# The second half's expert rows: gathered into buffers of their own and added by VectorE, instead of accumulated into x by the gather

## The chip, the cores and the metric

One NeuronCore of one Trainium2 chip runs one program. The metric is the device time of one execution in microseconds (us). Shorter is better.

## The reference, cut to what matters

Two transformer layers work on x of 8 batches by 512 tokens by 128 features, all in float32. Layer 0 adds to x a causal attention of 16 heads and a mixture of experts: every token goes to 6 of 32 experts, and a shared expert serves all. Layer 1 adds a second causal attention (4 heads) and a chain of three blocks of dense layers with a layer norm and a gelu.

```python
x = L0_attn_x
xn = _layernorm(x, axis=-1)
x = x + _L0_attn_ref(xn, ...) + _L0_ffn_ref(xn, ...)
xn = _layernorm(x, axis=-1)
x = x + _L1_attn_ref(xn, ...) + _L1_ffn_ref(xn, ...)

# in _L0_ffn_ref, TOP_K = 6
_, top_idx = jax.lax.top_k(corrected, TOP_K)
combine = jnp.zeros((T, E), x.dtype).at[jnp.arange(T)[:, None], top_idx].add(top_w)
out = jnp.einsum('teh,te->th', y, combine) + shared_out
```

Only the last sum of the mixture is touched here: for each token the weighted outputs of its six experts are added to x.

## The kernel before, in words

x stays on the chip as eight tiles `x_b[b]`, one for each batch, of 128 partitions by 4 token tiles by 128 features. The mixture is done in two halves of four batches each (`TH` = 16 token tiles a half). In each half GpSimd first scatters the rows of the normalised tokens to DRAM, grouped by expert (`scatter`, L605). `expert_slots` then works through them in 16 groups of 8 slots of 128 rows, and writes the weighted outputs to the DRAM tensor `ys[h]` (L691). Last, `gather` (L695) fetches them back: one indirect DMA of GpSimd brings, for a token tile `t` and a choice `k` of the six, 128 rows of 128 floats, and accumulates them into `x_b[b][:, tb, :]` in flight (`compute_op=ALU.add`). A half has 16 x 6 = 96 such gathers, ordered by batch, then choice, then token tile.

The order of the work is written by hand (`manual_schedule`): each engine executes its instructions in the order in which the program issues them. The main loop (L1138) runs over 193 ticks (`T1`), the steps of the change's title. Three ticks do the attention of a pair of heads: 64 pairs. In a tick stand, in this order: the scores of the next tick, the jobs planned for place 0, the exponentials, the transposes of the tick before, the jobs of place 1, a projection, in each third tick `values` (L512, the matmuls `yps`), and the jobs of places 2 and 3. `plan(tick, place, job)` puts a job into that order. After the loop a second one over `u` does layer 1, and works off the jobs of ticks `T1 + u`.

What is planned around the change:

- The second half's expert slots end at tick 145. Its gathers start at tick 149 (`FIRST_SLOTS[1] + APART * NG + 2` = 99 + 48 + 2), place 3, two a tick, and so end at tick 196. The first half's start at tick 101, three a tick.
- `output` (L580) adds batch b's attention to `x_b[b]`: 72 matmuls `z` on TensorE, then one VectorE instruction (L594). It is planned for place 3 of tick 24 (b + 1) + 13: 157 for batch 5, 181 for batch 6. Batch 7's stands at tick 194.
- `prepared(b)` (L831) brings x to layer 1 in eight steps: statistics on VectorE, powers and products on GpSimd (L153, L842, L845, L856, L874, L892, L899), transposes and projections on TensorE. Batches 0 and 1 are prepared from tick 150 on, a step every four ticks, at place 2 (`EARLY_AT`). The others come later; batch 4 starts at tick 195.
- `norm` (L1019) of the dense blocks also has its powers and products on GpSimd (L153, L1031).
- `divide` (L559) multiplies an attention output by its divisors on VectorE (L561, 128x512).
- `evacuate` (L157) gives each copy out of PSUM to VectorE or ScalarE, whichever has the smaller sum in `load_of`.
- `pp` is a pool of SBUF tiles that opens at tick 148, after the expert slots.

Of the kernel before, what the change touches and what calls it, by code (L numbers as in the profile page):

```python
# [10 lines left out]
F32 = mybir.dt.float32  # L11
# [3 lines left out]
ALU = mybir.AluOpType  # L15
AX = mybir.AxisListType

P = 128
B, L, D = 8, 512, 128
NT = L // P  # L20
# [9 lines left out]
TH = TT // NH  # L30
# [3 lines left out]
NG = NS // GS  # L34
FIRST_SLOTS, APART = (51, 99), 3
# [14 lines left out]
def kernel(ctx: ExitStack, tc: tile.TileContext, a: dict, out: bass.AP):  # L50
    nc = tc.nc
# [22 lines left out]
    rows = ctx.enter_context(tc.tile_pool(name="rows", bufs=1, space=bass.MemoryType.DRAM))  # L74
# [8 lines left out]
    x_b, x_in = [], a["x"].rearrange("b (t p) d -> b p t d", p=P)  # L83
# [47 lines left out]
    xs, ys = [], []  # L131
# [23 lines left out]
    load_of = {"dve": 0.0, "act": 0.0}  # L155
# [54 lines left out]
    index = w0.tile([P, TT, TOP_K], U32, name="index")  # L210
# [403 lines left out]
    def expert_slots(h, g):  # L614
# [77 lines left out]
            out=ys[h][at : at + GS * P].rearrange("(s p) d -> p s d", p=P), in_=yg  # L692
        )

    def gather(t, k):  # L695
        b, tb = divmod(t, NT)
        nc.gpsimd.indirect_dma_start(  # L697
            x_b[b][:, tb, :], None, ys[t // TH],
            bass.IndirectOffsetOnAxis(index[:, t, k : k + 1], 0), compute_op=ALU.add,
        )  # L700

    experts = ExitStack()

# [3 lines left out]
    def plan(tick, place, job, *args):  # L707
        beside.setdefault((tick, place), []).append((job, args))
# [33 lines left out]
    for h in range(NH):  # L742
        for g in range(NG):
            first = FIRST_SLOTS[h] + APART * g
            parts = expert_slots(h, g)

            for tick, place in ((-4, 3), (-3, 1), (-1, 1), (0, 2), (1, 3)):
                plan(first + tick, place, next, parts, None)
        moves = [
            (t, k) for b in range(h * B // 2, (h + 1) * B // 2) for k in range(TOP_K)  # L750
            for t in range(b * NT, (b + 1) * NT)
        ]
        for i, (t, k) in enumerate(moves):
            at = i // 3 if h == 0 else i // 2
            plan(FIRST_SLOTS[h] + APART * NG + 2 + at, 3, gather, t, k)

# [379 lines left out]
    for tick in range(T1):  # L1138
# [23 lines left out]
        if tick == FIRST_SLOTS[-1] + APART * NG + 1:  # L1162
            experts.close()
            token_rows[0].close()
            pp = later_pools.enter_context(tc.tile_pool(name="prep1", bufs=1, side="right"))
# [65 lines left out]
```

## Time and profile before

| | |
|---|---|
| time, median of 14 runs | 1391.99 us (1384.06 to 1399.53) |
| profiled execution's own time | 1393.89 us |
| its span, first to last instruction | 1392.2 us |
| mean granted TensorE clock | 0.904 of full speed |
| busy: TensorE / VectorE / ScalarE / GpSimd | 82% / 55% / 53% / 49% of the span |
| chain that ended last | PE 59%, issue 13%, POOL 13%, DVE 7%, DMA 2% |
| of it POOL, gathers (L697) | 7% |
| gathers, both halves | 192, 301.2 us busy on GpSimd |
| scatters, both halves | 192, 186.0 us busy on GpSimd |

The engines stand in the profile as PE (TensorE), DVE (VectorE), ACT (ScalarE), POOL (GpSimd) and SP (the engine whose queue issues most DMAs). [...] A group of instructions is written "line engine operation, output<-input". An idle time in square brackets is the time in which the engine stood still just before an instruction, with what ended it.

### The profile page before, as it was taken

To read this page: it belongs to the slowest core of one execution; us is meant where nothing else is said; L and a number is where in the kernel's file an instruction comes from. 1 tells how busy PE (TensorE), PEld (TensorE's weight loads), DVE (VectorE), ACT (ScalarE), POOL (GpSimd) and SP (SyncE) were. 2 spreads that over 40 slices of the span, in tenths; PEclk is the share of its full clock that TensorE was granted. 3 is DMA by queue.
4 is the path that set the end of the run, shared out by engine and by line. 5 is a ranking of instruction groups with operands and counts; after the bars stand their busy time and mean duration, and the time that the engine had idled before them with its cause. 6 is when DMAs were issued, how large, how long until landed. Compare 5 with 4: busy or idle time off the path is not lost.

```text
span 1392.2 us, 25274 instructions
## 1 busy us (share of the span) xinstructions
PE 1135.7 (82%) x8534; PEld 751.8 (54%) x8534; DVE 760.1 (55%) x2563; ACT 743.5 (53%) x1977; POOL 681.0 (49%) x738
## 2 busy tenths in 40 slices
PE   5897423942249999999999999999999777888896
PEld 2554211421225676667666666766656545665564
DVE  4572311600016656675665566566667357687885
ACT  4475211610006665675665566566556356677785
POOL 2037477187750000000058888402888878866651
PEclk9899655865559999999999999999999989999999
DMA  9529212131111465676679889852324224000000
GB/s 286 143 53 270 83 59 82 53 94 58 57 43 42 137 183 150 165 201 174 160 179 238 193 191 224 209 159 65 49 31 87 29 28 88 13 9 16 8 9 23
DMA packets 204052, 151.05 MB, mean 108 GB/s; under 512 B 17682, under 2 KB 192276, under 8 KB 203924
## 3 DMA queue, kind: packets, MB, share of 16 engines
q1 hardware_dynamic: 166340, 119.51, 31.5%
q0 software_dynamic: 36864, 28.34, 11.1%
q10 hardware_dynamic: 720, 1.61, 0.3%
q8 instruction: 67, 1.10, 0.3%
q14 instruction: 61, 0.50, 0.1%
HBM read 93.52 MB, written 55.87 MB: 107 GB/s over the span
## 4 chain that ended last, share of the span: by engine, by line
PE 59%; issue 13%; POOL 13%; DVE 7%; another core or an unknown queue 3%; DMA 2%; ACT 2%; SPq 0%; ACTq 0%; DVEq 0%; POOLq 0%
PE sc L457 11%; PE pt_ps L501 9%; PE yps L524 9%; POOL x L697 7%; PE qk_ps L427 7%; PE z L585 4%; PE v_ps L438 3%; PE ye_ps L679 2%; POOL rn L153 2%; PE xt_ps L655 2%; PE u_ps L667 2%; PE g_ps L667 2%; DVE neg L923 2%; PE pt_ps L956 1%
## 5 line engine op out<-in xcount | busy, mean ns | idle before, releaser
L697 POOL DMA_INDIRECT x<-ys,index x192 | 301.2, 1569 | 428.7 <-DMA ys<-yg 302.4
L465 DVE CUSTOM_DVE_ANT_0 neg<-sc,mask 128x512 f32<-128x512 f32 (+3 forms) x512 | 225.3, 486 | 166.6 <-PE sc L457 87.6
L480 ACT ACTIVATE neg<-neg,nmax 128x512 f32<-128x512 f32 (+3 forms) x512 | 281.3, 554 | 22.5 <-DVE nmax L465 22.3
L169 ACT COPY pT<-pt_ps 128x512 f32<-128x512 f32 x283 | 156.3, 585 | 256.2 <-PE pt_ps L501 179.7
L457 PE MATMUL sc<-qkT 64*128 64x384 f32 (+3 forms) x1024 | 206.1, 478 | 42.7 <-DVE nmax L465 21.8
L605 POOL DMA_INDIRECT xs<-xe,index x192 | 186.0, 969 | 62.0 <-issue 35.3
L501 PE MATMUL pt_ps<-ident,neg 128*128 128x128 f32 x1280 | 189.2, 287 | 26.6 <-issue 15.7
L501 PEld LDWEIGHTS pt_ps<-ident,neg 128*128 128x128 f32 x1280 | 141.0, 144 | 105.5 <-issue 55.0
L524 PE MATMUL yps<-pT,vs 128*64 128x128 f32 (+1 forms) x1792 | 162.0, 327 | 33.4 <-issue 27.4
L524 PEld LDWEIGHTS yps<-pT,vs 128*64 128x64 f32 x1792 | 113.1, 139 | 118.2 <-issue 63.2
L457 PEld LDWEIGHTS sc<-qkT 64*128 64x128 f32 x1024 | 91.7, 192 | 145.2 <-issue 58.4
L585 PE MATMUL z<-wz_sb,yT 128*128 128x128 f32 x512 | 80.0, 291 | 74.0 <-issue 72.8
L585 PEld LDWEIGHTS z<-wz_sb,yT 128*128 128x128 f32 x512 | 71.2, 204 | 83.7 <-issue 81.2
L480 ACT ACTIVATION_READ_ACCUMULATOR neg<-neg,nmax 128x1 f32 x512 | 97.8, 191 | 0.0
L163 DVE COPY pT<-pt_ps 128x512 f32<-128x512 f32 x117 | 76.8, 684 | 16.6 <-issue 8.0
L169 ACT COPY yT<-yps 128x512 f32<-128x512 f32 x42 | 24.6, 587 | 102.0 <-PE yps L524 72.3
L169 ACT COPY vs<-v_ps 128x512 f32<-128x512 f32 x47 | 27.6, 587 | 89.8 <-issue 61.1
L427 PE MATMUL qk_ps<-xnT,wk_sb 128*128 128x512 f32 x128 | 72.0, 646 | 2.7 <-ACT xnT L169 2.7
L594 DVE TENSOR_TENSOR x<-x,z 128x512 f32<-128x512 f32 x8 | 5.5, 687 | 124.0 <-PE sc L457 65.6
L561 DVE TENSOR_TENSOR yT<-yT,rb 128x512 f32<-128x512 f32 x64 | 46.3, 732 | 48.2 <-DMA rb<-sums 48.0
L937 ACT ACTIVATE neg<-neg,nmax 128x512 f32<-128x512 f32 (+3 forms) x128 | 70.2, 552 | 0.1
L427 PE MATMUL qk_ps<-xnT,wq_sb 128*128 128x512 f32 x128 | 69.4, 626 | 0.8 <-ACT xnT L169 0.7
(198 smaller groups left out, 1767.6 us busy)
## 6 DMA issues: line engine op xcount, KB each, us to landing
wx<-in_experts SPq DMA_DIRECT2D x256, 128.0 KB
xs<-zero SPq DMA_DIRECT2D x16, 1280.0 KB
xg<-xs SPq DMA_DIRECT2D x64, 320.0 KB
rb<-sums SPq DMA_DIRECT2D x128, 128.0 KB
ys<-yg SPq DMA_DIRECT2D x32, 512.0 KB
oh<-slot_rows SPq DMA_DIRECT2D x32, 128.0 KB
xs<-xe,index POOLq DMA_INDIRECT x192
x<-ys,index POOLq DMA_INDIRECT x192
```

Of the source, the lines that this page charges most:

```text
L163: nc.vector.tensor_copy(dst, src)
L169: nc.scalar.copy(dst, src)
L427: nc.tensor.matmul(ps, lhsT=w[:, c * P : (c + 1) * P], rhs=xnT[b], start=True, stop=True)
L457: nc.tensor.matmul(sc[j][:, off : off + w], lhsT=qT[r, i * P : (i + 1) * P], rhs=kT[r, :w], start=True, stop=True,)
L465: nc.vector.tensor_tensor_reduce(out=neg[:, j, off : off + w], in0=sc[j][:, off : off + w], in1=mask[:, L - w :], scale=-1.0, scalar=HUGE, ...
L480: nc.scalar.activation(neg[:, j, off : off + w], neg[:, j, off : off + w], AF.Exp, bias=nmax[:, 2 * k + j : 2 * k + j + 1], scale=-1.0, ac ...
L501: nc.tensor.transpose(ps[:, (start + k) * P : (start + k + 1) * P], pr[:, j, k * P : (k + 1) * P], ident,)
L524: nc.tensor.matmul(y[j * DK0 : (j + 1) * DK0, i * P : (i + hi - lo) * P], lhsT=vs[:, k, h * DK0 : (h + 1) * DK0], rhs=pt[:, j, lo:hi, :].r ...
L585: nc.tensor.matmul(z[:, t, :], lhsT=yts[b * NPAIR + c][:, (NT - 1 - t) * P : (NT - t) * P], rhs=wz[:, c, :], start=(c == 0), stop=False,)
L605: move = nc.gpsimd.indirect_dma_start(xs[h], bass.IndirectOffsetOnAxis(index[:, t, k : k + 1], 0), xe[h][:, t % TH, :], None,).ins
L697: nc.gpsimd.indirect_dma_start(x_b[b][:, tb, :], None, ys[t // TH], bass.IndirectOffsetOnAxis(index[:, t, k : k + 1], 0), compute_op=ALU.add,)
L937: nc.scalar.activation(neg[:, h, off : off + w], neg[:, h, off : off + w], AF.Exp, bias=nmax[:, H1 * k + h : H1 * k + h + 1], scale=-1.0, ...
```

## The change

The first half is left as it is. In the second half, the gathers of one choice `k` for one batch (four of them) go, without accumulation, into a tile `rows` of 128 x 4 x 128 floats, of which there are four buffers. A new job `collect` adds the tile to `x_b[b]` with one VectorE instruction of 128x512. It is planned three ticks after the last of the four gathers, at place 1: 24 instructions in all. `load_of["dve"]` counts 0.7 for each. The second half's gathers are planned at five in two ticks instead of four, so they end at tick 187, and the last `collect` stands at tick 190.

```diff
+    gathered = {}
+
     def gather(t, k):
         b, tb = divmod(t, NT)
+        dst, op = x_b[b], ALU.add
+        if t >= TH:
+            if tb == 0:
+                gathered[b, k] = pp.tile([P, NT, D], F32, name="rows", tag="rows", bufs=4)
+            dst, op = gathered[b, k], ALU.bypass
         nc.gpsimd.indirect_dma_start(
-            x_b[b][:, tb, :], None, ys[t // TH],
-            bass.IndirectOffsetOnAxis(index[:, t, k : k + 1], 0), compute_op=ALU.add,
+            dst[:, tb, :], None, ys[t // TH],
+            bass.IndirectOffsetOnAxis(index[:, t, k : k + 1], 0), compute_op=op,
         )
+
+    def collect(b, k):
+        nc.vector.tensor_tensor(x_b[b], x_b[b], gathered.pop((b, k)), ALU.add)
+        load_of["dve"] += 0.7
...
         for i, (t, k) in enumerate(moves):
-            at = i // 3 if h == 0 else i // 2
-            plan(FIRST_SLOTS[h] + APART * NG + 2 + at, 3, gather, t, k)
+            at = FIRST_SLOTS[h] + APART * NG + 2 + (i // 3 if h == 0 else i * 2 // 5)
+            plan(at, 3, gather, t, k)
+            if h == 1 and t % NT == NT - 1:
+                plan(at + 3, 1, collect, t // NT, k)
```

## The prediction

> **What bounds the kernel now.** I read the page first: TensorE is busy for 82% of the span and carries 59% of the chain that ended last, GpSimd 13%, and the gathers of L697 alone 7%. They matter only where GpSimd is late, so the next view is the groups by line. Columns: count, then busy us and mean ns of one, then idle time before.
>
> ```profile
> L697 POOL DMA_INDIRECT x<-ys,index x192 | 301.2, 1569 | 428.7 <-DMA ys<-yg 302.4
> L605 POOL DMA_INDIRECT xs<-xe,index x192 | 186.0, 969 | 62.0 <-issue 35.3
> L561 DVE TENSOR_TENSOR yT<-yT,rb 128x512 f32<-128x512 f32 x64 | 46.3, 732 | 48.2 <-DMA rb<-sums 48.0
> ```
>
> An accumulating gather costs GpSimd 1.57 us; a plain indirect DMA of as many rows (the scatter) 0.97 us. VectorE's product of two SBUF tiles of 128x512, the form of the new `collect`, takes 0.73 us.
>
> The second table is the busy time of each engine by stretches of the second half's gathers (954.8 to 1213.9 us).
>
> ```profile
> 1060.00:1080.00 20.00, 20.00 (x145) 12.64 (x144) 15.93 (x55) 14.02 (x39) 17.70 (x14) 1.00 0.50 104
> 1100.00:1120.00 20.00, 7.22 (x49) 5.57 (x49) 1.86 (x5) 3.17 (x6) 15.90 (x13) 0.78 0.24 28
> 1160.00:1180.00 20.00, 13.76 (x87) 9.79 (x84) 18.56 (x73) 15.47 (x40) 17.32 (x14) 0.91 0.57 134
> ```
>
> Columns: PE, PEld, DVE, ACT, POOL, then granted clock. Until 1080 us TensorE is full although GpSimd is loaded to 17.7 of 20 us: the gathers cost nothing there. From 1100 to 1120 only GpSimd works. From 1160 on VectorE is nearly full.
>
> The third view is the timeline of the engines across the hole (TensorE, VectorE, GpSimd):
>
> ```profile
> 1102.51 0.39 PE L589 MATMUL z<-wsd_sb,hs 128*128 128x128 f32 x2
> 1119.49 2.68 PE L457 MATMUL sc<-qkT 64*128 64x384 f32 x8 [12.78 <-DVE nmax L465]
> ```
> ```profile
> 1085.19 0.23 DVE L890 TENSOR_SCALAR rn<-rn,tscale 128x16 f32<-128x16 f32 x1 [3.34 <-POOL rn L153]
> 1087.16 0.68 DVE L561 TENSOR_TENSOR yT<-yT,rb 128x512 f32<-128x512 f32 x1
> 1118.14 0.69 DVE L594 TENSOR_TENSOR x<-x,z 128x512 f32<-128x512 f32 x1 [20.38 <-DMA x<-ys,index]
> ```
> ```profile
> 1087.24 2.05 POOL L697 DMA_INDIRECT x<-ys,index  x1 [0.30 <-issue]
> 1112.52 1.54 POOL L697 DMA_INDIRECT x<-ys,index  x1 [0.30 <-issue]
> 1114.37 1.54 POOL L697 DMA_INDIRECT x<-ys,index  x1 [0.30 <-issue]
> ```
>
> The last `z` of batch 6 (tick 181) is done at 1102.9 us. Its addition to `x_b[6]` on VectorE waits until 1118.14, because the gathers ordered before it accumulate into the same tile and GpSimd is late: 15.2 us. Behind that addition stand the score evictions L465, and behind those TensorE. One gather follows another every 1.54 + 0.30 = 1.85 us; in the chain of waits the transfer of the one started at 1114.37 carries the end until 1117.66, 1.75 us after its 1.54:
>
> ```profile
> 1114.37 3.29 DMA x<-ys,index
> 1117.69 0.05 DVEq L594
> ```
>
> **The change, part by part.**
>
> *The price of a plain gather* is in no row. From above: the accumulating gather, a period of 1.85 us. From below: the scatter, 0.97 plus the gap of 0.30, 1.27 us. Below that I see no row. I take 1.27: both handle 128 rows by an index, and what is dropped, the addition, is what the scatter does not have either. The software queue's packets agree: 730 in 20 us with 16 scatters issued (46 each) against 1467 with 11 gathers (133 each), so the accumulating one is chopped row by row.
>
> ```profile
> q0 software_dynamic: 730, 1.23, 19.6%
> q0 software_dynamic: 1467, 0.67, 27.8%
> ```
>
> [...]
>
> *What goes.* `output(6)` no longer waits for gathers: 15.2 us. After the hole the granted clock is 0.78 to 0.88, and the first scores and projection take 2.68 and 1.92 us instead of the 1.14 and 1.02 of earlier ticks: 2.4 us. At 1085.19 VectorE had waited 3.34 us for a power (`rn`) that stood behind gathers; with shorter gathers that power is early: 3.3 us. Together 20.9 us.
>
> *What is added: waits of `collect`.* VectorE now stops at a `collect` until its four gathers have landed; score evictions and copies queue behind it, then TensorE. So how late is GpSimd? It executes between 4-tick steps of `prepared` now 10 gathers, 12.7 us, in place of 8, 14.8 us. In the trace `yps` starts at 1006.82 in tick 159 and at 1054.30 in tick 171: 15.8 us for four ticks. With GpSimd's own 1.5 to 5 us beside the 12.7 it keeps step until tick 170. There the powers are long: `rn` (VectorE feeds it at about 1053.5) 4.24 and `sqk` 1.44 give 1059.4; ten gathers to 1072.1; at tick 174 `qn`, `kn` and the next `rn`, 7.5 us, to 1079.6 (the order needs them before 1067). The gathers of ticks 174 to 177 follow. A gather lands 0.97 + 1.75 = 2.7 us after its start. So the `collect` of tick 175 (last gather started 1067.0) waits 0.7 us; that of tick 177 (started 1079.8, landed 1082.5; VectorE is there at about 1076.3) 6.2; those of 178 and 180, behind an `lin_rstd` and `yn` of 2.7 us, 1.5 and 1.0. Sum 9.4 us. The 8.1 us of `z` at tick 181 then let GpSimd catch up, and only 16 gathers remain where 32 did. Lower bound 0 (if VectorE runs later than I set it), upper 9.4 plus 4.7 for a landing as slow as in the first half, where a gather had to wait 7.4 us for an earlier one.
>
> *What is added: 24 additions* of 0.7 us, 16.8 us of VectorE. Between 976 and 1100 us VectorE is busy two thirds of the time and TensorE is full, so most are covered. `load_of` also moves copies to ScalarE. Bounds: 0, and all 16.8 if each stands before a score eviction that TensorE waits for. Nearest row: TensorE waited on VectorE for scores four times in this stretch, twice for under a microsecond. I take a fifth, 3.4 us. If TensorE gets ahead and that cover is gone, it is the 16.8.
>
> *Contention.* The gather beside L561 above took 2.05 us instead of 1.54. A `collect` reads two SBUF tiles too. Six of them lie in the late stretch of ticks 170 to 180: 0 to 6 x 0.5 = 3.0 us; I take half, 1.5.
> [...]
>
> *After tick 183* GpSimd has fewer gathers (at 1215 us TensorE waited 2.3 + 0.5 us for `qn` and `kn` behind some), but six `collect`s, 4.2 us, fall partly into the stretch where VectorE is at 18.56 of 20. I set this at nothing; bounds -4 to +3.
>
> *Sum.* 20.9 - 9.4 - 3.4 - 1.5 = 6.6 us. The profiled execution took 1393.9 us, so 1387.3; it lies 1.9 above the median of 1392.0, from which 6.6 gives **1385.4**. With the bounds: best 20.9 + 3 = 24 us off, worst 20.9 - 14.1 - 16.8 - 3.0 - 4 = 17 us more. With the middle values each a few us off, the likely case spans 1376 to 1390.
>
> **The rivals.**
>
> *The plain gather costs what the accumulating one does (slower).* Place: GpSimd from 971 us to the last `collect`. Then 93 gathers x 1.855 = 172.5 us, plus GpSimd's other work: 971.35 to 1133.7 less 70 gathers x 1.855 = 32.5 us, and 2.8 for ticks 185 to 187. The last gather ends at 1179 and the `collect` of tick 190 waits for it until about 1182. Now tick 190 is at about 1152 (`yps` of 189 at 1149.43), so 30 us late; what GpSimd is later spared gives some 4 back. Plus 26: 1418. It decides from a period of about 1.39 us: between 1.27 (-6.6) and 1.855 (+26) the time is even there. For it: no row of a plain gather exists. Against: the scatter and the packets.
>
> *The additions lie on the path (slower).* Price: 16.8 instead of 3.4, and late landings, 4.7: 18 us worse than my sum, plus 12, 1404. It decides if more than 10 of the 16.8 us (3.4 + 6.6) show. Against: TensorE is full, VectorE is not.
>
> *The stall only moves.* The 20 us hole is spread over the `collect`s, since they too are late, and the 20.9 come back as waits: 1391. For it: GpSimd is the same engine and its order is the same.
>
> *The change does not do what it says*, in that the gathers wait for a free buffer: four buffers take 16 gathers, and a `collect` frees one about 6 gathers after its last, so none should. If they did, GpSimd would go at VectorE's pace, and the time would be that of the moved stall, 1391.
>
> **How the numbers follow.** My case 0.57 (1376 to 1390), the old price 0.15 (1405 to 1430), additions on the path 0.11 (1396 to 1410), moved stall 0.17 (1387 to 1396). 0.3%, 4.2 us, is about what a measurement of this kernel tells from no change. Faster than 1387.8: 0.49 of mine and 0.02 of the moved stall, 0.51. Slower than 1396.2: 0.15, 0.10 and 0.01, 0.26. Between: 0.23. A range of 1374 to 1407 leaves out most of the old price (0.13), some of the additions (0.04) and the tails of mine (0.03).
>
> **What would show it.** Right: L697 has two prices, 1.55 us for the first 96 and about 0.97 for the second; no wait of L594 for gathers; new waits of the additions for DMA at ticks 175 to 180, up to 6 us; the last gather near 1130 us; TensorE's hole at 1106 gone. Wrong: the second 96 still near 1.5 us, or waits of the additions that total more than 15 us, or TensorE waiting for VectorE in most ticks of 976 to 1100.

## The result, and the profile after

The changed kernel takes 1413.05 us (median of 10 executions, 1407.08 to 1419.48) where the kernel before, beside it on the same chip, takes 1389.97 (47 executions). The ratio is 1.0159, with a 95% interval of 1.0138 to 1.018: 1.6% slower, 22.1 us by the ratio. The forecast was 6.6 us faster, with a range that ended at 1407. Both the sign and the range were wrong. The profiled execution took 1414.03 us, its span is 1412.3, and its mean granted clock 0.898 (0.904 before).

First the page of the changed kernel: the chain that ended last by engine, the two groups of gathers, and the software queue. The line numbers have moved: L706 is the gather, L712 the new addition.

```profile
PE 65%; issue 12%; DVE 9%; another core or an unknown queue 5%; DMA 3%; ACT 2%; POOL 2%; SPq 0%; DVEq 0%; POOLq 0%; ACTq 0%
...
L706 POOL DMA_INDIRECT x<-ys,index x96 | 149.7, 1559 | 335.3 <-DMA ys<-yg 304.7
...
L706 POOL DMA_INDIRECT rows<-ys,index x96 | 95.7, 997 | 108.6 <-DVE nmax L465 67.6
```
```profile
q0 software_dynamic: 26112, 28.34, 8.8%
```

The price of a plain gather is what was forecast: 997 ns, and with the gap of 0.30 a period of 1.25 to 1.27 us. The queue's packets fell from 36,864 to 26,112. A stretch with scatters alone (300 to 380 us of the kernel before) has 2,736 packets for 57 of them, 48 each; one with plain gathers alone (1132 to 1143 us here) has 256 for eight, 32 each. What is left of the 36,864 is 144 for each accumulating gather. GpSimd's share of the chain fell from 13% to 2%. But "another core or an unknown queue" rose from 3% to 5%, TensorE from 59% to 65%. This program has one core, so "unknown" deserves to be opened.

The busy time by stretch, columns as in the prediction (PE, PEld, DVE, ACT, POOL, then granted clock, DMA share, GB/s):

```profile
1040.00:1060.00 20.00, 13.65 (x61) 6.83 (x59) 8.71 (x24) 8.32 (x28) 10.02 (x10) 0.74 0.12 32
1060.00:1080.00 20.00, 20.00 (x123) 12.17 (x121) 16.00 (x45) 12.68 (x37) 5.08 (x6) 1.00 0.07 20
...
1100.00:1120.00 20.00, 19.87 (x105) 11.14 (x104) 14.90 (x47) 14.08 (x38) 17.09 (x16) 0.83 0.22 70
...
1140.00:1160.00 20.00, 17.31 (x93) 10.29 (x94) 11.88 (x36) 11.53 (x30) 3.77 (x4) 0.83 0.06 17
```

The hole of 1100 to 1120 is gone: TensorE is busy for 19.87 us there, where it was for 7.22. There is a new, shallower one from 1040 (13.65, where TensorE was busy for all 20 us before). From 1140 on the busy time is what it was (17.31 and 17.35), but the clock is 0.83 where it was 1.00. GpSimd is not full in these two stretches either (10.02 and 3.77 of 20 us).

The waits of VectorE between 950 and 1250 us (line waited for, what ended the wait, us in total, times, longest). "remote" is a wait whose end nothing in the profile explains:

```profile
DVE x L594 <- remote: 14.1, 1, 14.1
DVE xnT L163 <- remote: 13.4, 1, 13.4
...
DVE neg L465 <- remote: 7.6, 5, 4.1
...
DVE pT L163 <- remote: 3.4, 1, 3.4
...
DVE x L712 <- DMA rows<-ys,index: 1.2, 1, 1.2
```

No wait of L594 for gathers is left, and the additions wait 1.2 us for theirs. In their place stand 38.5 us of waits without a named end. Before, this stretch had none. Not all of the 38.5 is loss, since a producer's own time is in a wait too.

The longest of them in the timeline of the changed kernel (start, us, engine; in brackets the idle time before and what ended it):

```profile
1133.11 0.69 PE L589 MATMUL z<-wsd_sb,hs 128*128 128x128 f32 x2
...
1142.69 2.54 PE L457 MATMUL sc<-qkT 64*128 64x384 f32 x5 [5.05 <-DVE x L594]
```
```profile
1141.34 0.69 DVE L594 TENSOR_TENSOR x<-x,z 128x512 f32<-128x512 f32 x1 [14.11 <-remote]
```
```profile
1140.18 0.94 POOL L706 DMA_INDIRECT rows<-ys,index  x1 [0.30 <-issue]
1141.43 0.94 POOL L706 DMA_INDIRECT rows<-ys,index  x1 [0.30 <-issue]
```

This is the same instruction as in the hole of before, batch 6's addition of `z`. It now depends on TensorE alone, whose last `z` ends at 1133.8. It starts 7.5 us after that, over half of its wait of 14.1. From 1132.60 to 1142.37 GpSimd issues eight plain gathers, one every 1.25 to 1.31 us. The 13.4 us wait looks the same: four transposes `tp` end by 1038.4, the copy of them starts at 1046.25, 7.9 us after that, and an unbroken row of gathers ends at 1044.94. So in both an engine stands still although what it waits for was done, by the modelled ends of the matmuls, and does so while plain gathers run back to back.

**The same thing was in the trace of before**, in a place that the prediction never opened: the scatters, from which it took its price. Of the kernel before, waits of VectorE from 90 to 420 us, two stretches of that time (columns as above), and two rows of the page (tenths in 40 slices, about 35 us each):

```profile
DVE neg L465 <- remote: 47.9, 7, 18.5
DVE yT L163 <- remote: 45.3, 1, 45.3
```
```profile
300.00:340.00 40.00, 9.31 (x25) 6.63 (x24) 2.30 (x6) 0.00 (x0) 30.57 (x58) 0.50 0.18 60
340.00:380.00 40.00, 10.01 (x27) 7.61 (x27) 0.69 (x1) 1.57 (x5) 30.53 (x57) 0.50 0.18 58
```
```profile
PE   5897423942249999999999999999999777888896
...
POOL 2037477187750000000058888402888878866651
```

While GpSimd issues scatters every 1.27 us, TensorE is busy for a quarter of the time at half its clock, and VectorE waits for nothing that can be named. In the first half's accumulating gathers (slices 21 to 25, period 1.85 us) TensorE is full.

### The profile page after: what moved, and what is told of

The parts are those of the page before. It is cut to its first block, busy times and chain, and to the rows that moved or that the text cites. A ratio compares the mean times of both kernels' runs of the same rounds, so it can differ in the third digit from the quotient of the medians.

```text
span 1412.3 us, 25325 instructions
## 1 busy us (share of the span) xinstructions
PE 1151.4 (82%) x8534; PEld 759.9 (54%) x8534; DVE 768.2 (54%) x2574; ACT 748.9 (53%) x1990; POOL 625.9 (44%) x738
## 4 chain that ended last, share of the span: by engine, by line
PE 65%; issue 12%; DVE 9%; another core or an unknown queue 5%; DMA 3%; ACT 2%; POOL 2%; SPq 0%; DVEq 0%; POOLq 0%; ACTq 0%
PE sc L457 12%; PE pt_ps L501 11%; PE yps L524 10%; PE qk_ps L427 8%; PE z L585 5%; PE v_ps L438 3%; PE ye_ps L679 2%; PE g_ps L667 2%; PE xt_ps L655 2%; PE u_ps L667 2%; DMA xg<-xs 2%; DVE neg L938 2%; POOL rn L153 1%; PE pt_ps L971 1%
## 5 line engine op out<-in xcount | busy, mean ns | idle before, releaser
L465 DVE CUSTOM_DVE_ANT_0 neg<-sc,mask 128x512 f32<-128x512 f32 (+3 forms) x512 | 225.8, 486 | 182.8 <-PE sc L457 85.1
L706 POOL DMA_INDIRECT x<-ys,index x96 | 149.7, 1559 | 335.3 <-DMA ys<-yg 304.7
L457 PE MATMUL sc<-qkT 64*128 64x384 f32 (+3 forms) x1024 | 211.9, 483 | 44.4 <-issue 26.1
L501 PE MATMUL pt_ps<-ident,neg 128*128 128x128 f32 x1280 | 193.6, 290 | 35.0 <-issue 32.2
L501 PEld LDWEIGHTS pt_ps<-ident,neg 128*128 128x128 f32 x1280 | 144.4, 146 | 115.9 <-issue 75.2
L706 POOL DMA_INDIRECT rows<-ys,index x96 | 95.7, 997 | 108.6 <-DVE nmax L465 67.6
L163 DVE COPY pT<-pt_ps 128x512 f32<-128x512 f32 x115 | 75.9, 685 | 21.3 <-remote 10.0
L438 PE MATMUL v_ps<-wv_sb,xnT 128*128 128x512 f32 x128 | 69.0, 624 | 2.8 <-issue 2.8
```

The costliest lines, as they stand in the source:

```text
L163: nc.vector.tensor_copy(dst, src)
L438: nc.tensor.matmul(ps, lhsT=xnT[b][:, t * P : (t + 1) * P], rhs=wv[:, g * 512 : (g + 1) * 512], start=True, stop=True,)
L457: nc.tensor.matmul(sc[j][:, off : off + w], lhsT=qT[r, i * P : (i + 1) * P], rhs=kT[r, :w], start=True, stop=True,)
L465: nc.vector.tensor_tensor_reduce(out=neg[:, j, off : off + w], in0=sc[j][:, off : off + w], in1=mask[:, L - w :], scale=-1.0, scalar=HUGE, ...
L501: nc.tensor.transpose(ps[:, (start + k) * P : (start + k + 1) * P], pr[:, j, k * P : (k + 1) * P], ident,)
L706: nc.gpsimd.indirect_dma_start(dst[:, tb, :], None, ys[t // TH], bass.IndirectOffsetOnAxis(index[:, t, k : k + 1], 0), compute_op=op,)
```

## The experiments

The theory after the result (A): plain indirect DMAs that GpSimd issues without a pause hold up the other engines, whatever they bring. The rival (B): the additions, or waits of the additions for late gathers, cost VectorE the time, and the unnamed waits only hide that.

One fact of the runs is needed to read them. The kernel before takes 1390 to 1396 us on some chips, and 1174 to 1176 us on others; the former are called affected here. Kernels compared with each other below ran on one chip, with the kernel before beside them. The five groups below ran on five chips, two affected and three not; the comparison above is from an affected one. Each of the five was measured in one session, so the runs can't tell a lasting property of a chip from its state at that time. Where an expectation gives times for one kind of chip and the run met the other, only its ratios and its waits can be compared.

**1. On an unaffected chip (before: 1175.71 us).** The gather's price, the pace and the additions, each alone.

`e1_plain_into_x`, from the kernel before:
```diff
-            bass.IndirectOffsetOnAxis(index[:, t, k : k + 1], 0), compute_op=ALU.add,
+            bass.IndirectOffsetOnAxis(index[:, t, k : k + 1], 0),
+            compute_op=ALU.add if t < TH else ALU.bypass,
```


> The kernel before, with the second half's gathers plain (no accumulation) and still straight into x, two a tick; the sum over the six experts is left out for that half. No buffers, no additions, no denser plan. Theory A (plain indirect DMAs that follow each other every 1.25 us hold up what the other engines signal to each other): waits of VectorE and ScalarE that end by nothing the profile can name, 15 us or more between 950 and 1180 us, where the kernel before has none; GpSimd does 56 us less, but the time is 1385 or more. Theory B (the 24 additions, the four buffers or five gathers in two ticks cause the loss): no such waits, the hole at batch 6 is short or gone, 1370 to 1380 us.

Measured: 1160.91 us, ratio 0.9881 (0.984 to 0.9922), 14.0 us faster. No wait without a named end, anywhere, and none of L594 for gathers. Its scatters are those of the kernel before: 977 ns each and 0.31 us between them, a period of 1.29 us, against 969 ns and 1.27 us. Here no wait of TensorE for another engine or a DMA totals more than 0.8 us beside them (60 to 400 us), and the mean granted clock of the execution is 0.988.

`e2_acc_into_rows`, from the changed kernel: buffers and additions stay, the gathers accumulate again, into zeroed buffers.
```diff
-            dst, op = gathered[b, k], ALU.bypass
+                nc.vector.memset(gathered[b, k], 0.0)
+            dst = gathered[b, k]
```


> The changed kernel, with the rows tiles zeroed by VectorE and the gathers accumulating into them; same buffers, additions and plan. Theory A: the unnamed waits are gone; instead GpSimd is late at 1.85 us a gather and the additions wait for gathers (DMA rows<-ys), which by the arithmetic of the prediction's first rival gives 1405 to 1420 us. Theory B: the unnamed waits stay and those for gathers come on top, 1425 or more.

Measured: 1201.66 us, 1.0226 (1.0189 to 1.0263), 26.6 us slower. The additions now wait for gathers:

```profile
DVE x L713 <- DMA rows<-ys,index: 54.3, 19, 5.2
```

The prediction's first rival said plus 26. That it is met so closely is partly luck: the interval runs from 22 to 31 us, the chip is another kind, and 24 fills of VectorE are new in this kernel. It is not what happened to the change.

`e3_plain_spaced`, from the changed kernel: GpSimd fills a tile of 128x512 after each plain gather, which makes the period 1.66 us.
```diff
+        if t >= TH:
+            nc.gpsimd.memset(pp.tile([P, NT, D], F32, name="space", tag="space", bufs=1), 0.0)
```


> The changed kernel, with a GpSimd memset of 128x512 (0.52 us in the profile before) after each plain gather of the second half, so that they follow each other every 1.9 us or so, as the accumulating ones did. If the pace is what holds the others up: no unnamed waits, the additions wait for gathers instead, 1400 to 1420 us. If it is the plain form at any pace: unnamed waits of 15 us or more remain, 1415 or more.

Measured: 1182.34 us, 1.0051 (1.0026 to 1.0076). The additions wait 31.6 us in 12 places: at this pace GpSimd is late.

`e4_batch6_apart`, from the kernel before: only batch 6's gathers go, still accumulating, into a zeroed tile of their own, added once at tick 197.
```diff
+    apart = {}
...
+        if b == 6 and not apart:
+            apart[b] = pp.tile([P, NT, D], F32, name="rows", tag="rows")
+            nc.gpsimd.memset(apart[b], 0.0)
...
-            x_b[b][:, tb, :], None, ys[t // TH],
+            apart.get(b, x_b[b])[:, tb, :], None, ys[t // TH],
...
+    def collect(b):
+        nc.vector.tensor_tensor(x_b[b], x_b[b], apart.pop(b), ALU.add)
...
+    plan(197, 1, collect, 6)
```


> The kernel before, accumulating as before, but batch 6's 24 gathers go into one tile that GpSimd zeroes, added to x by one VectorE instruction at tick 197. It removes the one wait that the prediction priced (VectorE's addition of batch 6 waiting for gathers, 15.2 us plus 2.4 us of slow clock) and nothing else. If that price is right: no hole at 1106 us, 1374 to 1380 us. If GpSimd's lateness only shows at the next step that needs it: 1386 to 1392 us.

Measured: 1171.13 us, 0.9958 (0.9936 to 0.9979), 4.9 us faster, nearer to the second expectation than to the first. The wait of L594 for gathers is gone, and the next thing to be late is a power of GpSimd's, in VectorE's timeline of this kernel:

```profile
955.21 0.16 DVE L861 TENSOR_TENSOR ms<-mv,rstd 128x4 f32<-128x4 f32 x1 [9.12 <-POOL rstd L153]
```

What follows: on this chip neither theory's loss exists, so these four sizes belong to the sum of the prediction, not to the loss. The loss had to be sought on an affected chip.

**2. On an affected chip (before: 1395.86 us).** The changed kernel again; the kernel before again, for its trace; the changed kernel with its gathers at the old rate of the plan; and the scatters, which the change does not touch, made slow.

> The changed kernel once more, unchanged, since the kernel before took 1175.7 us in the first four experiments where it had taken 1390.0 in the comparison of the change, and no profile of the first four has an unnamed wait, not even around the scatters. Theory A1 (plain indirect DMAs hold the others up on the chip of the comparison only): on a chip where the kernel before takes about 1176, no unnamed waits, and the arithmetic of the prediction holds: 5 to 15 us faster than before. On a chip where it takes about 1390, unnamed waits of 35 us or so and 1.6% slower. Theory B (the change's own additions and plan cost the time, and the unnamed waits are a symptom): 1 to 2% slower on either.

Measured: 1423.88 us, 1.0191 (1.016 to 1.0223). Unnamed waits of VectorE in the second half's gathers: 36.6 us.

> The kernel before, for its profile on the same chip. Theory A1: where it takes about 1176 us, no unnamed waits between 60 and 400 us either, where the scatters are; where it takes about 1390, about 100 us of them on VectorE there, as in the first profile. The hole at batch 6 (VectorE waiting about 20 us for gathers) is there on either.

Measured, one execution: 1394.59 us, span 1392.9. Around the scatters VectorE's waits without a named end are led by L465 with 59.6 us and L163 with 51.4; L594 waits 20.3 us for gathers at the hole.

`c2_two_a_tick`, from the changed kernel:
```diff
-            at = FIRST_SLOTS[h] + APART * NG + 2 + (i // 3 if h == 0 else i * 2 // 5)
+            at = FIRST_SLOTS[h] + APART * NG + 2 + (i // 3 if h == 0 else i // 2)
```


> The changed kernel with the second half's gathers planned two a tick, as before the change, the additions still three ticks after the last of four. It undoes the density alone. If five in two ticks is what makes the additions wait: 3 to 8 us faster than the changed kernel on the same chip, and the waits of the additions for gathers shrink to nothing. If not: within 3 us of it. Where unnamed waits exist they stay, since the gathers still follow each other every 1.25 us in groups of eight.

Measured: 1412.53 us, 1.0099 (1.0066 to 1.0132). The unnamed waits of VectorE fall from 36.6 to 17.5 us, the time by 11.4. Neither case of the expectation was met: the gain is larger, the unnamed waits did not stay, and the waits of the additions for gathers did not shrink (3.5 us, against 0.9 in `c2_after`). It is half a cure, presumably since fewer gathers are planned in a tick, but they still follow each other every 1.25 to 1.33 us (four of them from 1045.51 to 1049.37 us).

`c2_scatter_add`, from the kernel before: the scatter accumulates into `xs`, which the kernel zeroes anyway. It takes GpSimd 1.57 us instead of 0.97.
```diff
         nc.gpsimd.indirect_dma_start(
...
+            compute_op=ALU.add,
```


> The kernel before with the scatters accumulating into their DRAM tensor, which the kernel has set to zero before, so that the sum is the same; nothing else. It makes the 192 scatters of the accumulating form. Theory A: on a chip with unnamed waits around the scatters these vanish and the kernel gains 30 to 150 us; on a chip without them it loses, or gains nothing: GpSimd needs 0.6 us more for each, 115 us in all, in a stretch where TensorE is full, so 1176 to 1190. Rival (the unnamed waits have nothing to do with the form): they stay, and the time is that of the kernel before or more.

Measured: 1223.39 us, ratio 0.8752 (0.8723 to 0.878): an instruction that is 62% dearer makes the kernel 12.5% faster, 172 us and so more than the 150 that were expected at most. No wait without a named end is left. Page of this kernel, the group of the scatters and the rows in tenths:

```profile
PE   5897999957999999999999999999995978788886
...
POOL 2008999989989980038888830178898788767641
...
L605 POOL DMA_INDIRECT xs<-xe,index x192 | 301.9, 1572 | 36.5 <-issue 36.1
```

In slices 5 to 12 TensorE read 2 to 4 in the kernel before, but for one 9; here it reads 9, but for a 5 and a 7, with GpSimd fuller than it was. B has no place for this: no addition is touched.

**3. On another affected chip (before: 1392.43 us).** Is it the pace, or the accumulating form? Plain DMAs are kept and only spaced.

The kernel of `e3_plain_spaced` again:

> The changed kernel with a GpSimd memset after each plain gather, as before; on the unaffected chip it made a period of 1.66 us. On an affected chip (kernel before about 1390): if the pace is what holds the others up, the unnamed waits between 950 and 1180 us fall from 35 us on VectorE to under 10, and the time is 1395 to 1405, what GpSimd's lateness costs. If the plain form does it at any pace: 20 us or more of them and 1410 to 1425. On an unaffected chip it only repeats 1.005.

Measured: 1397.21 us, 1.0028 (1.0005 to 1.005), against 1.0144 for the changed kernel on this chip. GpSimd's timeline of this kernel, and the one kind of wait that VectorE has left in the gathers:

```profile
1000.72 0.95 POOL L706 DMA_INDIRECT rows<-ys,index  x1 [0.17 <-issue]
1001.67 0.55 POOL L711 MEMSET space<- 128x512 f32 x1
1002.38 0.95 POOL L706 DMA_INDIRECT rows<-ys,index  x1 [0.17 <-issue]
```
```profile
DVE x L714 <- DMA rows<-ys,index: 26.0, 9, 4.3
```

At 1.66 us no unnamed wait is left after 780 us. What remains is named, and costs about what it cost on the unaffected chip (1.0051).

`c3_scatter_spaced`, from the kernel before: three small fills after each scatter instead of one.
```diff
-        nc.gpsimd.memset(small.tile([P, 1], F32, name="gap", tag="gap", bufs=1), 0.0)
+        for _ in range(3):
+            nc.gpsimd.memset(small.tile([P, 1], F32, name="gap", tag="gap", bufs=1), 0.0)
```


> The kernel before with three small memsets after each scatter instead of one, so that plain scatters follow each other every 1.8 us, the pace of accumulating ones; form unchanged. On an affected chip: if pace decides, the unnamed waits around the scatters go as they went with accumulation, 1210 to 1250 us; if form decides, they stay and the time is 1380 to 1400. In between: both count. On an unaffected chip: within 10 us of before.

Measured: 1221.99 us, 0.8764 (0.8742 to 0.8787). Its timeline of GpSimd, and the largest unnamed waits from 90 to 420 us:

```profile
121.46 0.96 POOL L605 DMA_INDIRECT xs<-xe,index  x1
122.42 0.43 POOL L610 MEMSET gap<- 128x1 f32 x3
123.00 0.96 POOL L605 DMA_INDIRECT xs<-xe,index  x1
```
```profile
DVE neg L465 <- remote: 8.0, 4, 3.7
DVE yT L163 <- remote: 7.4, 1, 7.4
```

The period is 1.54 us, not the 1.8 that I expected of three fills, and that is already enough for nearly all of it: 21.7 us of VectorE's unnamed waits remain. So 0.27 us more between two DMAs of the same form are worth 170 us here, and the form alone is not the cause.

`c3_best`: the accumulating scatters and batch 6 apart, in one kernel.

> The kernel before with accumulating scatters, and batch 6's accumulating gathers in a zeroed tile added at tick 197. On an affected chip: the 0.875 of the accumulating scatters, and 4 to 6 us less for the hole, as on the unaffected chip: 1216 to 1222 us where the kernel before takes 1390 to 1396. On an unaffected chip: 1175 to 1190, a loss for the scatters as GpSimd is late with them.

Measured: 1216.67 us, 0.8731 (0.871 to 0.8751).

> The changed kernel unchanged. On an unaffected chip (kernel before about 1176) theory A says that the prediction's arithmetic holds: 5 to 15 us faster and no unnamed waits. Theory B: 10 to 25 us slower there too. On an affected chip it only repeats 1.016 to 1.019, and serves the others as their base.

Measured: 1415.22 us, 1.0144 (1.01 to 1.0187); unnamed waits of 41.4 us.

**4. On another unaffected chip (before: 1174.2 us).** What does the change bring where nothing is held up, and can a paced version keep it?

> The changed kernel unchanged. On an unaffected chip (kernel before about 1176): no unnamed waits and 5 to 15 us faster, if the prediction's sum is right apart from the hold-up; 10 to 25 us slower if the additions and the plan cost the time. On an affected chip a repeat: 1.014 to 1.019.

Measured: 1161.18 us, 0.9892 (0.9864 to 0.992): **12.7 us faster** (9.4 to 16.0). There is no wait without a named end, with gathers of 947 ns (median) at the same 1.25 us. The additions' waits of this kernel, and the longest of them:

```profile
DVE x L712 <- DMA rows<-ys,index: 8.9, 5, 3.8
```
```profile
864.10 0.69 DVE L712 TENSOR_TENSOR x<-x,rows 128x512 f32<-128x512 f32 x1 [3.79 <-DMA rows<-ys,index]
```

`d1_scatter_spaced4`: the kernel before with four fills after each scatter (as above, `range(4)`).

> The kernel before with four small memsets after each scatter, a period of about 1.7 us. Theory: at 1.54 us unnamed waits of about 18 us on VectorE were left around the scatters, at 1.66 us none around the gathers; so none here, and 1205 to 1225 us on an affected chip. On an unaffected one within 10 us of before. It is the base for the next two.

Measured: 1203.64 us, 1.0257 (1.0216 to 1.0298). It is 30 us slower where at most 10 were expected. TensorE waits 13.3 us for scatters: pacing has its own price.

`d2_after_spaced`: the changed kernel with these four fills, and three after each plain gather.

> The changed kernel with scatters as in d1_scatter_spaced4 and three small memsets after each plain gather of the second half (period about 1.55 us). If the hold-up was all that the prediction missed, its sum with GpSimd at 1.55 instead of 1.27 us holds against d1_scatter_spaced4: between 7 us faster (the forecast) and 12 us slower (half way to the 26 us that it gave for 1.855). If the additions and the plan have a price of their own: 15 us or more slower.

Measured: 1206.33 us, 1.0282 (1.0253 to 1.0312), 2.7 us above `d1`. The additions wait 29.0 us.

`d3_after_spaced_late`, from `d2`:
```diff
-                gathered[b, k] = pp.tile([P, NT, D], F32, name="rows", tag="rows", bufs=4)
+                gathered[b, k] = pp.tile([P, NT, D], F32, name="rows", tag="rows", bufs=5)
...
-            at = FIRST_SLOTS[h] + APART * NG + 2 + (i // 3 if h == 0 else i * 2 // 5)
+            at = FIRST_SLOTS[h] + APART * NG + 2 + (i // 3 if h == 0 else i // 2)
...
-                plan(at + 3, 1, collect, t // NT, k)
+                plan(at + 6, 1, collect, t // NT, k)
```


> As d2_after_spaced, with the gathers two a tick, the additions six ticks after the last of four gathers instead of three, and five buffers instead of four. If the additions' waits for gathers are what is left of the loss, they go, and the kernel is 5 to 15 us faster than d1_scatter_spaced4. If not, within 4 us of d2_after_spaced.

Measured: 1182.58 us, 1.0071 (1.0044 to 1.0098): 21.1 us below `d1`, more than the 5 to 15 expected, and no addition waits for a gather. The thinner plan, the later additions and the fifth buffer were changed together, so their shares are not told apart.

**5. On a third unaffected chip (before: 1175.8 us).** Two kernels without an unpaced plain DMA: `f1_spaced_both` is `d3` with three fills after a scatter instead of four; `f2_accumulating_both` is the kernel of `c3_best`.

> As d3_after_spaced_late (plain gathers spaced by three small memsets, two a tick, additions six ticks later, five buffers), but three memsets after a scatter instead of four: 1.54 us, which left 18 us of unnamed waits on VectorE and did not make the scatters late. On an affected chip it beats both kernels: about 1222 us of the spaced scatters less the 20 us that d3 was under d1, 1195 to 1210. On an unaffected one 1160 to 1180.

Measured: 1170.23 us, 0.995 (0.9925 to 0.9975).

> Accumulating scatters and batch 6 apart, on the same chip as f1_spaced_both. On an affected chip 1215 to 1220 as before, 10 to 20 us above f1_spaced_both. On an unaffected one 1190 to 1215, since there the late scatters made TensorE wait 11 to 13 us at a period of 1.7 us and these stand at 1.86.

Measured: 1215.0 us, 1.034 (1.0292 to 1.0388), above the 1175 to 1190 that `c3_best` was expected to take on an unaffected chip. With the same scatters TensorE waited 23.4 us for them in `c2_scatter_add`. The kernel of `f2_accumulating_both` took 1216.67 us on an affected chip. Without plain DMAs at full pace the two chips, 217 us apart for the kernel before, are 2 us apart.

**What is shown and what is not.** Shown, on two affected chips: plain indirect DMAs every 1.25 to 1.27 us come with waits that nothing named ends, 36.6 and 41.4 us of VectorE's time in the changed kernel's gathers (`c2_after`, `c3_after`). Shown on one of them: a pace of 1.66 us in the gathers and 1.54 in the scatters takes them away or nearly so, with the same form, the same data and the same additions. B is refuted: its additions are in `c3_plain_spaced` and `d4_after`; in the first 0.28% is left of the loss, in the second nothing. The pace was slowed by fills in between or by the dearer form; a pause without an instruction in it was not tried. Not shown is what is late inside the chip. That it is the signal from one engine to another is inferred from the timeline of the changed kernel, where the consumer starts 7.5 and 7.9 us after the producer's modelled end. Nor does any run show why only some chips have these waits. `f1_spaced_both` was not run on an affected chip.

No kernel here was shown to be better than the kernel before and the changed one on both kinds of chips. Where chips are affected, `c3_best` is the fastest that was run (12.7% below the kernel before); where they are not, it is 3.4% slower than the kernel before, and the change itself is the fastest that computes all (1161.18).

## Why the prediction was wrong, point by point

**The price of a plain gather: the failed step.** Its number was right (1.27 us forecast, 1.25 to 1.27 measured, `e2` confirming what the old price would have cost). But the step took a row's duration on its own engine for the whole price of the operation. The scatter row, from which it came, stood in a stretch in which TensorE was busy for 9 of 40 us and VectorE waited 93 us for nothing named. The prediction read three views of the gathers' stretch and none of the scatters'. The bound "below that I see no row" spoke of GpSimd alone; the price on the others was bounded nowhere and stood at nothing in the sum, and in the profile of the changed kernel it stands as 38.5 us of VectorE's waits. The two kinds of chips give its size, if all else is equal on them: 22.1 us slower with the unnamed waits (20.0 and 26.7 in the two later comparisons on affected chips), 12.7 faster without, so about 35 us.

**What goes: right in kind, too large.** The waits of L594 for gathers are gone on every chip. On an unaffected chip this part alone (`e1`) is worth 14.0 us (9.2 to 18.8) where the sum had 20.9.

**Waits of the additions: size right, price too high.** 8.9 us in `d4_after`, longest 3.8, for a forecast of 9.4, longest 6.2. The place was right too: they stand before the additions of ticks 174, 175, 177, 178 and 180 (0.9, 0.7, 3.8, 2.4, 1.2), where the forecast had 0.7, 6.2, 1.5 and 1.0 from tick 175 on. On the affected chips they total 0.9 to 7.4, presumably because VectorE itself is late there. But they were all put on the path. The 7.4 us of the upper bound stands in no row: in the trace of before the longest wait of a gather for an earlier one is 0.80 us, and 7.4 is the time of four gathers. **The additions and contention** were set at 3.4 and 1.5. The row behind the 3.4 was misread: from 976 to 1100 us TensorE waited on VectorE for scores twice (0.82 and 1.58 us), not four times; the four are those of a longer stretch, with the hole's 12.8 us among them. `d4` and `e1` together say that waits, additions and contention cost about 1 us (14.0 less 12.7) and not 14.3; the two ran on different chips and their intervals overlap, so that this is a size, not a proof. What contention costs was not shown: in `d4_after` single gathers take up to 1.49 us where the median is 0.95, and single additions up to 1.89 where the median is 0.69, and no run shows what made these long.

**The sum.** On a chip without the effect, the change brings 12.7 us, twice the forecast 6.6. There the sign was right, but the size only came as near as it did because a gain set 7 us too high stood against costs set 13 us too high.

**Free buffers.** "None should" wait for one. On the affected chip GpSimd waited 14.1 us, three times, for an addition to free a buffer: VectorE stood in unnamed waits ahead of it. On the unaffected one (`d4_after`) it waited 0.6. Likewise "the last gather near 1130": the last starts at 1169.60.

**The rivals.** The old price was about right as arithmetic (`e2`), and did not happen. The additions on the path: refuted by `d4`. The moved stall is seen in `e4`, where taking away the wait brought 4.9 of the 17.6 us that were put down to it and the clock after it; the plain gathers bring more, presumably because they make GpSimd's later powers early as well: from 700 to 1050 us VectorE waits 16.0 us for powers in `e4` and 3.6 in `e1`. What did happen is a fourth mechanism on the slower side, and none of the rivals was near it.

## What to carry to other kernels

Where an operation's price is taken from a neighbouring row, look at what all other engines did while that row ran, and open every wait whose end the profile can't name, above all where a program has one core. A faster instruction on an engine off the path also raises a rate, and here, on the affected chips, the rate of plain indirect DMAs, not their number or form, decided over 12% of the time (the same 192 scatters every 1.54 us instead of every 1.27: 1221.99 us instead of 1392.43). Compare on more than one chip before a change of this kind is accepted or thrown out: this one gains 1.1% on the one unaffected chip that it ran on and loses 1.4 to 1.9% in three comparisons on affected ones.

## What the runs showed of the hardware that was not expected

- On two of the five chips of the experiments, and in the comparison, plain indirect DMAs at a period of 1.25 to 1.27 us came with waits of the other engines that nothing named ends: 38.5 us of VectorE's in the gathers of the changed kernel in the comparison, 36.6 in `c2_after`, 41.4 in `c3_after`. Beside the scatters the granted clock of TensorE was 0.50 (300 to 380 us, in the kernel before of the comparison and in `c2_before`). With scatters every 1.54 us 21.7 us of VectorE's unnamed waits are left (`c3_scatter_spaced`); with gathers every 1.66 us (`c3_plain_spaced`, after 780 us) and with accumulating scatters every 1.86 us (`c2_scatter_add`) none. The kernel before runs at 1390 to 1396 us on such chips and at 1174 to 1176 on the others.
- An indirect DMA of 128 rows costs GpSimd 1.57 us and 144 packets as an accumulating gather (kernel before), and 1.57 us as an accumulating scatter (`c2_scatter_add`); plain, the gather costs 1.00 us and 32 packets (changed kernel), the scatter 0.97 us and 48 (kernel before).
- Three small fills of GpSimd (128x1) take 0.43 us together (`c3_scatter_spaced`), one of 128x512 takes 0.55 (`c3_plain_spaced`).
